# Leftover tap coefficients of a convolution in a two-layer graph network: from a block table to sixteen 32x32 products

## The chip, the cores and the metric

The kernel runs on one core of one Trainium2 chip. The metric is the device time of one execution in microseconds (us). Three runs of the kernel before gave a median of 1967.43 us (1967.24 to 1968.04).

A core has TensorE (PE in the profile, its loads of stationary weights PEld), VectorE (DVE), ScalarE (ACT), GpSimd (POOL) and SyncE (SP). SP computes nothing here: it issues most of the DMA transfers, in the order in which the program gives them, and stands still when one has to wait.

## The reference

Two layers on 128 graphs of 128 nodes with 256 features each, all in float32. The first layer mixes each graph with its adjacency matrix and ends in a layer norm. The second has a branch with two convolutions along the nodes, a message-passing branch, a GRU cell and a layer norm. The change concerns the second convolution, conv2_w with 256 x 256 channels and 17 taps:

```python
xc = jnp.transpose(x, (0, 2, 1))
h = _bn(_conv1d(xc, conv1_w, 0), bn1_g, bn1_b, bn1_m, bn1_v)
h = jax.nn.relu(h)
h = _bn(_conv1d(h, conv2_w, 8), bn2_g, bn2_b, bn2_m, bn2_v)
x_conv = jnp.transpose(jax.nn.relu(h + xc), (0, 2, 1))
```

## The kernel before

**The convolution by frequencies.** The kernel makes the 17-tap convolution from cosine and sine coefficients of length L = 136 (128 nodes and 8 of padding). So there are M = 136 real coefficients for each input and each tap filter: 128 main ones and ML = 8 leftover ones. A table T holds the cosines and sines at the 17 lags, one row a lag, in each quarter of the 128 partitions (rows 0, 32, 64 and 96 on). The coefficients of the filters are W[m] = sum over the taps of T[tap, m] * w[tap], for every pair of input and output channel. They go to memory in w_d, one 512 KB block for each pair of coefficients.

**Stages.** Three stages follow each other.
- The first, up to about 660 us, runs 64 rounds, t = 0 to 63, over pairs of graphs (a_round). A round projects one pair through the first layer (l0_project: f_ps, gate_ps), finishes earlier pairs (gate, norm), runs the first convolution of an older pair (l1_front: conv_ps), takes its coefficients (l1_analyse: coef_ps), turns the next pair's features (l0_turn: xT, adj_ps) and mixes with the adjacency (l0_mix: mix_ps). At its end stand the filter coefficients: a w_unit or a v_unit, or nothing.
- The second loads w_d block by block and multiplies it with the coefficients of the inputs (y_ps, z_ps).
- The third does the rest of the second layer, from synthesis to the GRU (conv2_ps, g_ps).

**Order.** In the first stage the order on TensorE, SP, VectorE, ScalarE and GpSimd is the order of the program text (manual_schedule). PSUM has eight banks, handed out in turn (bank).

**Main units.** A unit u handles four input channels of each of the two input halves, one channel in each quarter of the partitions. w_load(u) loads its taps with four transfers of 64 KB into one of NW = 2 buffers (wt). w_unit(u) makes four products, one in each row group of 32 rows: 17 rows, the 128 main columns of T as stationary weights, 512 moving columns (256 outputs of each half). Four copies on ScalarE empty the four banks into w_o, and w_store writes 1 MB to w_d in the next round. There are NU = 32 units, in rounds 2, 4, ... 32, 33, 35, ... 63; the last one is run after the rounds. The taps for unit u + 2 are loaded in the round after unit u.

**Leftover units.** For the 8 leftover coefficients the taps are loaded a second time. v_load brings FS = 7 input channels with their 17 taps into 119 rows of vt. A block table TL, put together in rounds 3 to 9 by 14 small transfers (leftover_table), has T's eight leftover columns once for each of the 7 channels, on its own 17 rows. v_unit is then one product of 128 rows, 128 columns and 512 moving columns, of which 56 output rows count; VectorE copies them to wl_o, and v_store writes them with two transfers in packets of 2 KB. There are NV = 19 such units, spread over rounds without a main unit.

**What else the prediction names.** SP's list in a round is, in this order: in odd rounds four loads of the next two pairs (xb, load_blocks), one store of the finished features (x_d, x1_store), one load of features (x, load_x), one of the adjacency (adjT, load), the stores of a unit, four loads that bring back the stored features in another layout (x1b, load_back), one store of the turned features (x1T_d, x1T_store), and at the end the taps (w_load). The turn of xb into xT on VectorE is wanted by the next round's f_ps; the turn of x1b into x1T (l1_turn) is wanted by conv_ps.

Of the kernel before, what the change touches and what calls it, by code (L numbers as in the profile page):

```python
# [14 lines left out]
P = 128  # L15
D = 256
# [18 lines left out]
def gnn_layers_kernel(ctx: ExitStack, tc: tile.TileContext, a: dict, out: bass.AP):  # L35
# [53 lines left out]
    FS = P // TAPS  # L89
    TL = taps.tile([P, P], F32, tag="TL", name="TL")  # L90
# [5 lines left out]
    vt = taps.tile([P, 2, D], F32, tag="vt", name="vt")  # L96
# [183 lines left out]
    def way_back():  # L280

        AL = setup.tile([P, P // ML, ML], F32, tag="AL", name="AL")
        nc.vector.tensor_copy(AL, A[:, P:M].unsqueeze(1).to_broadcast([P, P // ML, ML]))
        nc.gpsimd.memset(TL, 0.0)

        nc.gpsimd.memset(vt[96:], 0.0)
        back = setup.tile([P, 1], F32, tag="back", name="back")
        nc.gpsimd.memset(back, 2.0 / L)
        nc.gpsimd.memset(back[0:2], 1.0 / L)
        yield  # L290
        tS = bank("S_ps")
        nc.tensor.transpose(tS[:, 0:P], A[:, 0:P], ident)
        nc.tensor.transpose(tS[:, P : 2 * P], AL.rearrange("p a b -> p (a b)"), ident)
        nc.vector.tensor_scalar(S, tS[:, 0:P], back, None, ALU.mult)
        nc.vector.tensor_scalar(SL, tS[:, P : 2 * P], 2.0 / L, None, ALU.mult)

    def leftover_table(i):

        cols = TL[:, 0 : ML * FS].rearrange("p (r i k) -> p r i k", r=2, i=FS)
        for r in range(2):  # L300
            nc.sync.dma_start(cols[i * TAPS : (i + 1) * TAPS, r, i, :], T[0:TAPS, P + r : M : 2])
# [191 lines left out]
    NV = -(-P // FS)  # L493
    s_v = {}

    def v_set(v):

        return FS * v, min(FS, P - FS * v)

    def v_load(v):  # L500
        f, n = v_set(v)
        nc.sync.dma_start(
            vt[0 : n * TAPS],
            a["conv2_wT"].rearrange("(c f) t o -> (f t) c o", c=NC)[f * TAPS : (f + n) * TAPS],
        )

    def v_unit(v):
        pl = bank(f"wl_ps_{v}")
        nc.tensor.matmul(  # L509
            pl, lhsT=TL, rhs=vt.rearrange("p i (o c) -> p i c o", c=NC), start=True, stop=True  # L510
        )
        ol = s_v[v] = taps.tile([ML * FS, NC * D], F32, tag="wl", name=f"wl_o_{v}")
        nc.vector.tensor_copy(ol, pl[0 : ML * FS])

    def v_store(v):
        ol = s_v.pop(v)
        f, n = v_set(v)
        h = ML // 2
        for r in range(2):
            nc.sync.dma_start(  # L520
                w_d[P // 2 : M // 2, r, f : f + n].rearrange("k f c o -> f k (c o)"),
                ol[r * h * FS : r * h * FS + n * h],
            )

# [41 lines left out]
    units = {2 + 2 * u - 2 * u // NU: u for u in range(NU)}  # L566
    rest = [t for t in range(4 + FS, NP - 1) if t not in units]
    units_v = {rest[v * (len(rest) - 1) // (NV - 1)]: v for v in range(NV)}
# [8 lines left out]
    def a_round(t):  # L577
# [25 lines left out]
        if t + 2 < NP:  # L603
            if 2 <= t + 2:
                load(t + 2)
            if 3 <= t < 3 + FS:
                leftover_table(t - 3)
            if t == FS:
                v_load(0)
# [5 lines left out]
        if t - 1 in units_v:  # L615
            v_store(units_v[t - 1])
            if units_v[t - 1] + 1 < NV:
                v_load(units_v[t - 1] + 1)
# [26 lines left out]
        if 0 <= t < 2:  # L645
            w_load(t)
        if t - 1 in units and units[t - 1] + NW < NU:
            w_load(units[t - 1] + NW)
        if t in units_v:
            v_unit(units_v[t])  # L650
        if t in units:
            if t + 1 < NP:
                w_unit(units[t])

    with tc.manual_schedule(engines={E.PE, E.SP, E.DVE, E.Activation, E.Pool}):
# [5 lines left out]
        w_unit(units[last])  # L661
# [8 lines left out]
        w_store(units[last])  # L670
# [578 lines left out]
```

## Time and profile before

| what | value |
|---|---|
| median of three runs | 1967.43 us |
| profiled execution | 1967.16 us |
| its span, first to last instruction | 1965.4 us |
| granted TensorE clock, mean | 0.997 |
| busy: VectorE, ScalarE, GpSimd | 1501.1, 737.5, 672.8 us |
| w_ps records on TensorE (line 482) | 256 |
| wl_ps records on TensorE (line 509) | 38, 612 ns each (median) |
| copies of w_ps on ScalarE (line 485) | 128, 597 ns each |
| copies of wl_ps on VectorE (line 513) | 19, 670 ns each |
| loads of vt | 18 of 238 KB, 1 of 68 KB |
| stores of wl_o | 36 of 56 KB, 2 of 16 KB |
| loads of wt | 127 of 64 KB, 1 of 34 KB |

A float32 product appears in the profile as two weight loads and two matmul records, its two passes. The records of TensorE overlap, so the busy time of a group is more than what it adds to the span; the distance from the start of one product to the start of the next tells that. In the table of windows a line has the window in us, its length, then for each engine the busy time with the number of instructions in brackets, the granted clock, the busy share of the DMA engines and their GB/s. In the timeline a line has the start, the length from the first to the last of the merged instructions, and their number. The chain of waits follows the work that ended last back from the end. SPq is the instruction stream of SP.

### The profile page before, as it was taken

The page shows a single profiled execution, that of the slowest core. Times are in us where ns is not written, and L with a number is a line of the kernel's source. Part 1 is how long each engine was busy: PE and PEld are TensorE (multiplying, and loading weights), DVE is VectorE, ACT ScalarE, POOL GpSimd, SP SyncE. Part 2 cuts the span into 40 slices and gives each one's busy share as a digit, 9 for nine tenths or more (in the row PEclk, how much of TensorE's full clock was granted, in tenths as well). Part 3 has the DMA queues.
Part 4 walks back from the last instruction along what each step waited for, and adds up shares of the span by engine and source line. Part 5 has one row for each costly group of instructions (what it writes and reads, how often), then busy time and mean ns, then how long its engine had stood idle before and what let it go on. Part 6 is the DMA issues. An engine that isn't in the chain of part 4 may idle for free.

```text
span 1965.4 us, 26741 instructions
## 1 busy us (share of the span) xinstructions
PE 1940.7 (99%) x8539; PEld 1325.4 (67%) x8539; DVE 1501.1 (76%) x3035; ACT 737.5 (38%) x1489; POOL 672.8 (34%) x887
## 2 busy tenths in 40 slices
PE   8999999999999999999999999999999999999997
PEld 5666666666666888866666666666666666666664
DVE  8888888888888644477787777777778777787776
ACT  4666666666666311122223322222222232222222
POOL 2111111111111355544344434434433452543431
PEclk9999999999999999999999999999999999999999
DMA  6787878877786899963212212221221222221100
GB/s 172 204 239 213 238 211 235 242 223 227 217 235 191 278 320 336 313 196 93 66 57 80 82 55 70 72 71 60 82 76 49 72 82 69 62 76 39 43 28 22
DMA packets 334660, 279.90 MB, mean 142 GB/s; under 512 B 150735, under 2 KB 276921, under 8 KB 334521
## 3 DMA queue, kind: packets, MB, share of 16 engines
q1 hardware_dynamic: 327817, 272.68, 45.6%
q10 hardware_dynamic: 6704, 5.52, 0.9%
q8 instruction: 69, 1.13, 0.2%
q14 instruction: 70, 0.57, 0.1%
HBM read 173.26 MB, written 104.86 MB: 142 GB/s over the span
## 4 chain that ended last, share of the span: by engine, by line
PE 93%; DVE 3%; DMA 1%; ACT 1%; issue 1%; POOL 1%; SPq 0%; ACTq 0%; POOLq 0%; DVEq 0%
PE g_ps L1116 43%; PE f_ps L353 11%; PE y_ps L799 5%; PE conv_ps L445 5%; PE gate_ps L358 5%; PE msg_ps L970 4%; PE coef_ps L466 3%; PE conv_ps L916 3%; PE z_ps L812 3%; PE nmp_ps L1048 3%; PE mix_ps L379 3%; PE w_ps L482 2%; PE wl_ps L509 1%; PE conv_ps L923 1%; PE adj_ps L333 1%
## 5 line engine op out<-in xcount | busy, mean ns | idle before, releaser
L318 ACT ACTIVATE y<-y,nb_b,rstd_b 128x256 f32<-128x256 f32 x128 | 70.0, 593 | 561.3 <-DVE nb_b L316 561.3
L353 PE MATMUL f_ps<-w,xT 128*128 128x512 f32 x512 | 244.6, 600 | 2.3 <-DVE xT L423 1.2
L1159 POOL TENSOR_TENSOR u<-u,p 128x512 f32<-128x512 f32 x63 | 79.9, 1269 | 249.1 <-DVE p L1139 240.4
L353 PEld LDWEIGHTS f_ps<-w,xT 128*128 128x128 f32 x512 | 89.1, 189 | 102.8 <-issue 79.8
L1116 PE MATMUL g_ps<-t_h,sh 128*128 128x384 f32 x384 | 156.8, 490 | 0.0
L1116 PE MATMUL g_ps<-t_c,sc 128*128 128x384 f32 x384 | 155.2, 486 | 0.0
L1116 PE MATMUL g_ps<-t_m,sm 128*128 128x384 f32 x384 | 155.2, 486 | 0.0
L358 PEld LDWEIGHTS gate_ps<-w,xT 128*128 128x128 f32 x512 | 97.2, 190 | 68.3 <-issue 53.6
L192 POOL TENSOR_SCALAR rstd_a<-mv_a 128x2 f32<-128x2 f32 x64 | 12.2, 191 | 354.3 <-DVE mv_a L309 249.7
L358 PE MATMUL gate_ps<-w,xT 128*128 128x256 f32 x512 | 131.5, 379 | 0.1
L799 PE MATMUL y_ps<-wb,H 128*128 128x256 f32 x544 | 128.4, 379 | 0.3 <-DMA wb<-w_d 0.3
L807 POOL TENSOR_TENSOR ws<-wb 128x512 f32<-128x512 f32 x67 | 94.4, 1411 | 88.6 <-PE z_ps L812 52.1
L445 PE MATMUL conv_ps<-conv_w,x1T 128*128 128x259 f32 x512 | 122.6, 381 | 0.6 <-DVE x1T L423 0.6
L362 ACT ACTIVATE hom<-f_ps,norm 128x256 f32<-128x256 f32 x128 | 60.6, 473 | 141.4 <-PE f_ps L353 141.3
L799 PEld LDWEIGHTS y_ps<-wb,H 128*128 128x128 f32 x544 | 103.3, 190 | 14.7 <-issue 0.7
L1075 ACT ACTIVATE o<-o 128x1024 f32<-128x1024 f32 (+1 forms) x65 | 67.6, 1040 | 113.7 <-POOL o L1160 54.5
L445 PEld LDWEIGHTS conv_ps<-conv_w,x1T 128*128 128x128 f32 x512 | 97.1, 190 | 16.0 <-PE w_ps L482 1.5
L1116 PEld LDWEIGHTS g_ps<-t_c,sc 128*128 128x128 f32 x384 | 73.0, 190 | 50.9
L1116 PEld LDWEIGHTS g_ps<-t_m,sm 128*128 128x128 f32 x384 | 73.0, 190 | 50.9 <-DVE sm L1064 0.3
L1116 PE MATMUL g_ps<-w_hhT_w,cx1T 128*128 128x384 f32 x256 | 105.1, 492 | 0.0
L1116 PE MATMUL g_ps<-w_ihT_w,nmpT 128*128 128x384 f32 x256 | 103.8, 487 | 1.2 <-ACT nmpT L1052 1.2
L1116 PE MATMUL g_ps<-w_ihT_w,xcT 128*128 128x384 f32 x256 | 103.6, 486 | 1.3 <-ACT xcT L937 1.3
(243 smaller groups left out, 4402.6 us busy)
## 6 DMA issues: line engine op xcount, KB each, us to landing
wb<-w_d SPq DMA_DIRECT2D x68, 512.0 KB
w_d<-w_o SPq DMA_DIRECT2D x32, 1024.0 KB
y_d<-yb SPq DMA_DIRECT2D x68, 256.0 KB
x<-in_x SPq DMA_DIRECT2D x64, 256.0 KB
x_d<-x SPq DMA_DIRECT2D x64, 256.0 KB
cx1T<-x1T_d SPq DMA_DIRECT2D x64, 256.0 KB
yt<-y_d SPq DMA_DIRECT2D x32, 512.0 KB
cx<-x_d SPq DMA_DIRECT2D x32, 512.0 KB
```

The lines of the kernel that those rows point to most:

```text
L318: nc.scalar.activation(dst[:, q, :], src[:, q, :], AF.Identity, bias=nb[:, q : q + 1], scale=rstd[:, q : q + 1],)
L353: nc.tensor.matmul(pf, lhsT=xT[:, c, nodes(j)], rhs=w0[:, c, 0 : 2 * D], start=(c == 0), stop=(c == NC - 1),)
L358: nc.tensor.matmul(pg[:, j * D : (j + 1) * D], lhsT=xT[:, c, nodes(j)], rhs=w0[:, c, 2 * D : 3 * D], start=(c == 0), stop=(c == NC - 1),)
L362: nc.scalar.activation(hom[:, j, :], pf[:, 0:D], AF.Copy, scale=norm[:, j : j + 1])
L379: nc.tensor.matmul(pm[:, j * D : (j + 1) * D], lhsT=adjT_[:, j, :], rhs=hom[:, j, :], start=True, stop=True,)
L445: nc.tensor.matmul(ph[:, 0 : D + CO], lhsT=s["x1T"][:, c, nodes(j)], rhs=conv1_w[:, c, :], start=(c == 0), stop=(c == NC - 1),)
L799: nc.tensor.matmul(py[:, blk, :], lhsT=coefs(blk if k == 0 else 2 * k + 1 - blk, c), rhs=w[:, blk, c, :], start=(c == 0), stop=(c == NC - 1),)
L807: nc.gpsimd.tensor_tensor(ws, w[:, 0], w[:, 1], ALU.add)
L970: nc.tensor.matmul(pm[:, pr * P : (pr + 1) * P], lhsT=s["fh"][i][:, pr, :], rhs=factors["g"][i], start=True, stop=True, skip_group_check=True,
L1075: nc.scalar.activation(rz, rz, AF.Tanh, scale=0.5)
L1116: nc.tensor.matmul(pg[:, lo : lo + 3 * P], lhsT=s[f"f{kind}"][i][:, pr, :], rhs=factors[kind][i], start=(k == 0), stop=(k == 2), skip_grou ...
L1159: nc.gpsimd.tensor_tensor(u4, u2, p5, add)
```

## The change

The leftover coefficients are no longer made from a table TL and taps of their own. They come from the tiles wt that the main units have loaded, for two units (a "set") at once. TL, vt, leftover_table, v_load and v_unit go.

v_set(i) runs sixteen products. For each unit e of the pair and each input half c there is a column group of 32 columns (g); in each row group r, 17 rows of T with its last 32 columns (104 to 135, the eight leftover ones last) are the stationary weights, and the 256 outputs of one half the moving columns. The four column groups of a row group write to the four quarters of the partitions of one bank. Four copies on ScalarE (128x256) bring the banks to wl_o, and v_store writes the eight rows that count of each quarter, with four transfers in packets of 1 KB.

```diff
-    FS = P // TAPS
-    TL = taps.tile([P, P], F32, tag="TL", name="TL")
-    vt = taps.tile([P, 2, D], F32, tag="vt", name="vt")
...
-        nc.gpsimd.memset(TL, 0.0)
-        nc.gpsimd.memset(vt[96:], 0.0)
...
-    def v_unit(v):
-        pl = bank(f"wl_ps_{v}")
-        nc.tensor.matmul(
-            pl, lhsT=TL, rhs=vt.rearrange("p i (o c) -> p i c o", c=NC), start=True, stop=True
-        )
-        ol = s_v[v] = taps.tile([ML * FS, NC * D], F32, tag="wl", name=f"wl_o_{v}")
-        nc.vector.tensor_copy(ol, pl[0 : ML * FS])
+    def v_set(i):
+        po = [bank(f"wl_ps_{i}_{r}") for r in range(Q)]
+        for e in range(2):
+            t = wt[(2 * i + e) % NW].rearrange("p i (o c) -> p i c o", c=NC)
+            for c in range(NC):
+                g = slice(K * (NC * e + c), K * (NC * e + c + 1))
+                for r in range(Q):
+                    k = slice(K * r, K * r + TAPS)
+                    nc.tensor.matmul(
+                        po[r][g, 0:D], lhsT=T[k, M - K : M], rhs=t[k, c], start=True, stop=True
+                    )
+        ol = s_v[i] = taps.tile([P, Q, D], F32, tag="wl", name=f"wl_o_{i}")
+        for r in range(Q):
+            nc.scalar.activation(ol[:, r, :], po[r][:, 0:D], AF.Copy)
+
+    def v_store(i):
+        ol = s_v.pop(i)
+        w = w_d.rearrange("k s (r u) c o -> u c (k s) r o", r=Q)
+        for e in range(2):
+            for c in range(NC):
+                lo = K * (NC * e + c) + K - ML
+                nc.sync.dma_start(w[2 * i + e, c, P:M], ol[lo : lo + ML])
...
-    units = {2 + 2 * u - 2 * u // NU: u for u in range(NU)}
-    rest = [t for t in range(4 + FS, NP - 1) if t not in units]
-    units_v = {rest[v * (len(rest) - 1) // (NV - 1)]: v for v in range(NV)}
+    units = {2 + 2 * u - (u > 10) - (u > 20): u for u in range(NU)}
+    sets = {t + 1: u // 2 for t, u in units.items() if u % 2}
...
-            if 3 <= t < 3 + FS:
-                leftover_table(t - 3)
-            if t == FS:
-                v_load(0)
...
-        if t - 1 in units_v:
-            v_store(units_v[t - 1])
-            if units_v[t - 1] + 1 < NV:
-                v_load(units_v[t - 1] + 1)
+        if t - 1 in sets:
+            v_store(sets[t - 1])
...
-        if 0 <= t < 2:
+        if 0 <= t < NW:
             w_load(t)
-        if t - 1 in units and units[t - 1] + NW < NU:
-            w_load(units[t - 1] + NW)
-        if t in units_v:
-            v_unit(units_v[t])
+        if t in sets and t + 1 < NP:
+            v_set(sets[t])
+            for e in range(2):
+                w_load(2 * sets[t] + NW + e)
         if t in units:
-            if t + 1 < NP:
-                w_unit(units[t])
+            w_unit(units[t])
...
-        w_unit(units[last])
+        v_set(sets[last])
...
-        w_store(units[last])
+        v_store(sets[last])
```

The units now stand in rounds 2, 4, ... 22, 23, 25, ... 41, 42, 44, ... 62, so the last one is inside the rounds. The sets stand in the round after each odd unit: 5, 9, 13, 17, 21, then 24, 28, 32, 36, 40, then 43, 47, 51, 55, 59, and the sixteenth, of round 63, is run after the rounds in the place of the last w_unit. Since a set reads both buffers of taps, the taps of the next two units are loaded after it, eight transfers at once; before, four were loaded after each unit.

## The prediction

> **What bounds the kernel now.** I read the page's shares first, then the slices, then the chain of waits, and last the table of busy time in single rounds.
>
> ```profile
> PE 1940.7 (99%) x8539; PEld 1325.4 (67%) x8539; DVE 1501.1 (76%) x3035; ACT 737.5 (38%) x1489; POOL 672.8 (34%) x887
> PE   8999999999999999999999999999999999999997
> PEclk9999999999999999999999999999999999999999
> ...
> PE 93%; DVE 3%; DMA 1%; ACT 1%; issue 1%; POOL 1%; SPq 0%; ACTq 0%; POOLq 0%; DVEq 0%
> ```
>
> TensorE is busy in every slice at its full clock, and 93% of the chain that ended last is its own work. The change lives in the first stage, up to about 660 us. There the time is a sum of rounds, so I cut out five rounds, each from the first f_ps product of one round to that of the next. The columns are window, length, and then the busy time of each engine.
>
> ```profile
> 163.33:173.45 10.12, 10.12 (x47) 6.53 (x45) 9.04 (x20) 5.39 (x13) 2.07 (x5) 1.00 0.60 172
> 173.45:182.79 9.34, 9.19 (x42) 6.36 (x39) 7.36 (x17) 7.36 (x17) 1.29 (x3) 1.00 0.85 251
> 182.79:192.99 10.20, 10.20 (x46) 6.62 (x46) 9.13 (x21) 5.42 (x14) 2.27 (x6) 1.00 0.64 185
> 192.99:202.92 9.93, 9.93 (x45) 6.90 (x42) 7.94 (x19) 7.39 (x17) 1.48 (x4) 1.00 0.92 273
> 202.92:213.04 10.12, 10.12 (x48) 6.53 (x46) 9.04 (x20) 5.40 (x13) 2.08 (x5) 1.00 0.70 184
> ```
>
> The second round holds neither a main unit nor a leftover unit (call it empty): 9.34 us. The third holds a w_unit: 10.20. The fourth holds a v_unit: 9.93. The first and fifth hold a w_unit after a round with a v_unit: 10.12. TensorE is full in all but the empty one, where it misses 0.15 us. Nothing waits for a DMA here, although the DMA engines are 60 to 92% busy. So the time of this stage moves with what stands on TensorE at the end of a round.
>
> **What is removed.** A v_unit is one 128x512 product in two passes:
>
> ```profile
> 201.15 1.03 PE L379 MATMUL mix_ps<-hom,adjT 128*128 128x256 f32 x4
> 202.02 1.06 PE L509 MATMUL wl_ps<-vt,TL 128*128 128x512 f32 x2
> 202.92 0.59 PE L353 MATMUL f_ps<-w,xT 128*128 128x512 f32 x1
> ```
>
> From its start to the next product is 0.90 us, but it is not worth that. In an empty round TensorE waits about a third of a microsecond for the turned xT before the next f_ps, and the v_unit fills that wait. By pairs of rounds, 9.93 + 10.12 with it against 9.34 + 10.20 without, it costs 0.51 us. Nineteen of them: 19 x 0.51 = -9.7 us. That is all that removal can bring on the path. The copies that go from VectorE (19 of 0.67 us), 19 loads of taps, 38 stores, 14 small table loads and two memsets early in the second round lie beside a full TensorE; I take 0 for them. Their ends: a gain of 0.5 us for the memsets (0.73 us of POOL at 25 us), no loss.
>
> **What is moved.** The 32 units stood in rounds 2 to 63, the last one behind the rounds, in a stretch where TensorE waits anyway (0.61 us idle after it, until x1T is turned). Now the last one stands in round 62, so one more round carries a w_unit: 10.20 - 9.34 = +0.86. In its old place stands the last of the sixteen sets. The gap there is 1.11 us of w_unit plus 0.61 idle, 1.7 in all; a set shorter than that is hidden: 0, and at the most 0.3 if it is the longest below.
>
> **What is added on TensorE.** Fifteen sets in rounds that would be empty, each sixteen products of 17 rows, 32 columns of weights and 256 moving columns. Four row groups, four column groups, two passes each: 32 matmul records. No row of the trace has fewer than 128 columns of weights, so the price has to be bounded. The nearest rows are the products in row groups alone (line 482, then line 1028):
>
> ```profile
> 172.34 1.18 PE L482 MATMUL w_ps<-wt,AT 17*128 17x512 f32 x8
> 173.45 0.70 PE L353 MATMUL f_ps<-w,xT 128*128 128x512 f32 x1
> ```
>
> ```profile
> 978.14 0.73 PE L1028 MATMUL dist_ps<-own,turned 32*128 32x128 f32 x16
> 978.80 0.91 PE L1116 MATMUL g_ps<-t_h,sh 128*128 128x384 f32 x2
> ```
>
> Eight records of 512 columns take 1.11 us until the next product starts. One pass of 512 columns is 0.43 us (four f_ps records in 1.72 us of the chain), so the four row groups run together: 2 x 0.43 = 0.86, and 0.25 for entering and leaving. Against an empty round a w_unit costs 0.86, its two passes and no more, since entry and exit fall into the wait for xT. In the second row each row group has two products, and 16 records of 128 columns (0.108 us a pass, half of the adj_ps pair's 0.22) take 0.66: four passes one behind the other, 0.43, and 0.23 around them. So products of one row group follow each other, where all share the same columns.
>
> A pass of 256 columns is 0.215 us (mix_ps: 0.86 / 4). Taking a set at its streaming time, as the w_unit is:
> - all sixteen tiles together: 2 x 0.215 = 0.43 us;
> - column groups one behind the other, as line 1028 shows for products that share their columns: 8 x 0.215 = 1.72;
> - between them: each row group takes its products in order, the two passes of one product can't overlap, but the first pass of a product runs beside the second pass of the one before it in other columns. Then 2 + 3 = 5 steps: 1.07.
>
> With no overlap at all it would be 32 x 0.215 = 6.9, which both rows exclude. I take 1.07: the rows show that products in different parts of the array overlap and that a row group works in order, and this value keeps both. Fifteen sets: 16.1 us, with ends 6.5 and 25.8.
>
> The Trainium skill, TensorE: Matmul & The Clock Gate (Part 3: Packing small matmuls), reports 10.6 times for sixteen 32x32 tiles of 512 columns; by it a set would take 6.9 / 10.6 = 0.65 us (an estimate from that page), fifteen sets 9.7, and the change would come out at nothing. No row here shows column groups, and the page's case has one pass a product where these have two.
>
> **What is added elsewhere.** Each set has four copies on ScalarE of 128x256 from PSUM (line 363 does this in 0.375 us): 1.5 us a set, at the start of a round whose ScalarE is busy 5.4 of 10.1 us and whose first other work (hom) starts 2.0 us into it. Hidden: 0; if that cover were gone, hom would be late by some tenths, and mix_ps, its reader, stands 8 us later. The Trainium skill, TensorEngine Tiling (Array Packing), PSUM Bottleneck, warns that packing moves the bottleneck to emptying PSUM. Here four w_o copies of 0.6 us already empty a w_unit's four banks in time, so I add nothing for it.
>
> The queue on SP: the two loads of taps for the next pair now wait for the set's last product, at the very end of the round, and everything later on SP stands behind them. One issue takes 0.46 us:
>
> ```profile
> 122.40 1.84 SPq L156 DMA_DIRECT2D wt<-in_conv_wT  x4
> ...
> 132.33 1.91 SPq L126 DMA_DIRECT2D xb<-in_x  x4
> 134.34 0.43 SPq L456 DMA_DIRECT2D x_d<-x  x1
> ```
>
> Eight issues, 3.7 us into the next round; the taps land 2 to 5 us later (2.00 for an x1b load, 5.00 for an x_d store in the chain) and are wanted by the w_unit at 9 us. In ten of the sets the rest of SP's round (x_d, x, adjT, four stores of leftovers in place of two, x1b) ends near 9 us, x1b lands at 11 to 14 and is turned near 13, its conv_ps product stands at 16: no stall. In the five sets of even rounds (24, 28, 32, 36, 40) the four xb loads of the next pair come behind the taps as well. They start at 3.7 us instead of -1, end at 5.6, land at 7.6 to 10.6; VectorE turns xT at 8.4 and TensorE needs it by 9.2. Between 0 and 1.4 us late, five times: 0 to +7. I take 0, from the landing of 2.00.
>
> **Sum.** The profiled execution took 1967.16 us (span 1965.4), the median of the runs is 1967.43, 0.27 above it. -9.7 + 0.86 + 16.1 + 0 = +7.3. From the profiled 1967.16 that is 1974.4; with the 0.27, 1974.7.
>
> **Rivals.**
> *All sixteen tiles run together.* -9.7 + 0.86 + 6.5 = -2.3: 1965.1, not slower. It decides as soon as a set costs less than 0.59 us ((9.7 - 0.86) / 15), the break-even point. For it: tiles share neither rows nor columns pairwise, and four row groups do start together in line 482. Against it: both passes of a product need the same tile, and line 1028 shows a row group working in order.
> *The column groups run one after another.* -9.7 + 0.86 + 25.8 + 0.3 = +17.3: 1984.7. For it: line 1028, the only row in which a row group has several products, is serial. Against: those share all 128 columns.
> *SP's queue decides.* The xb loads come late in the five even rounds, +7 at the most, on top of the least cost of the sets: 1972. For it: the eight issues stand directly ahead of them, and the DMA engines are up to 92% busy. Against: the w_unit that ends those rounds covers 0.8 us of a late xT.
> *The transfers saved bring time.* 4.5 MB of taps less to load. No wait of TensorE in the rounds ends on a DMA; this gives nothing and has no case of its own.
>
> **How the numbers follow.** Order within a row group, columns overlapping (with a set of 0.8 to 1.3 us): 0.40, 1971 to 1979. All together: 0.33. Serial columns: 0.20. SP's queue: 0.07. The likeliest gives 1974.7. The range takes in the two ends of the unknown price, 1965.1 and 1984.7: 1964 to 1985. About 0.2%, 3.9 us, is what a measurement of this kernel can tell from no change. Slower by more: the first case, serial columns, SP's queue, less a little for a set near 0.8: 0.63. All together falls mostly within the bound (0.24), and goes below it with a few gains beside it (0.13).
>
> **What would show it.** In the profile after, the rounds with a set against empty ones: 10.4 us if a set costs 1.07, 9.8 if 0.43, 11.1 if 1.72, and 9.34 still for empty rounds. The matmul records of the sets should start in five steps of about 0.215 us. SP should wait for the set's products ahead of the taps, and f_ps should wait for xT in rounds 25, 29, 33, 37 and 41 no longer than in empty ones; if it does, the queue was mispriced. A stage after 660 us that changes its length would refute the whole account, which leaves it as it was.

## The result and the profile after

The changed kernel takes 1971.45 us (median of 17 runs, 1968.58 to 1973.19), the kernel before in the same series 1967.61 (17 runs, 1966.35 to 1969.25). The ratio is 1.0017, with a 95% interval of 1.0010 to 1.0024: slower by 2 to 4.7 us, a little less than the prediction's bound of 0.2% (3.9 us). The profiled execution took 1969.42 us with a span of 1967.6, so it belongs to the faster half of its kernel's runs.

First the page of the changed kernel: busy times, two rows of the slices, the shares of the chain that ended last, and the group of f_ps products. The last two numbers of that group are the idle time of TensorE right ahead of it, and how much of that ended on xT.

```profile
PE 1937.3 (98%) x9013; PEld 1320.0 (67%) x9013; DVE 1491.3 (76%) x3016; ACT 757.6 (39%) x1553; POOL 671.3 (34%) x885
...
PE   8999999999999999999999999999999999999997
...
PEclk9999999999999999999999999999999999999999
...
PE 89%; DVE 5%; DMA 2%; ACT 1%; issue 1%; POOL 1%; SPq 1%; POOLq 0%; DVEq 0%; ACTq 0%
...
L341 PE MATMUL f_ps<-w,xT 128*128 128x512 f32 x512 | 246.5, 604 | 7.7 <-DVE xT L411 6.6
```

The same group in the kernel before:

```profile
L353 PE MATMUL f_ps<-w,xT 128*128 128x512 f32 x512 | 244.6, 600 | 2.3 <-DVE xT L423 1.2
```

The slices look as before: TensorE full, clock full. But of the chain TensorE has 89% in place of 93, VectorE 5 in place of 3 and DMA 2 in place of 1, and f_ps waits 6.6 us for xT where it waited 1.2. So there are new stalls, and they end on VectorE.

Rounds of the changed kernel, each from its first f_ps to the next round's (columns as in the prediction's windows): an empty round, one with a w_unit, one with a set, the one after the set, and an empty round in trouble.

```profile
153.28:162.61 9.33, 9.18 (x42) 6.35 (x39) 7.35 (x17) 7.37 (x17) 1.29 (x3) 1.00 0.99 289
162.61:172.81 10.20, 10.20 (x46) 6.61 (x46) 9.13 (x21) 5.42 (x14) 2.26 (x6) 1.00 0.54 161
172.81:182.59 9.78, 9.78 (x74) 6.56 (x70) 7.69 (x18) 7.40 (x17) 1.29 (x3) 1.00 0.96 282
182.59:192.82 10.23, 10.23 (x59) 6.64 (x46) 8.90 (x20) 6.58 (x17) 2.26 (x6) 1.00 0.52 143
302.56:313.45 10.89, 9.18 (x42) 6.35 (x39) 7.79 (x18) 7.14 (x17) 1.77 (x4) 1.00 0.80 236
```

The set round is 9.78 us, 0.45 above the empty one, and the w_unit round after it 10.23 instead of 10.20: a set is worth 0.48 us, not 1.07. TensorE is full in it (9.78 of 9.78). The last line is round 30: the same work as the empty round, 9.18 us of busy TensorE, but 10.89 long. The rounds longer than their kind are 24, 26, 30, 34, 38, 42 and 61, by 0.22, 0.19, 1.56, 1.49, 0.52, 0.71 and 0.40 us: 5.1 together. Five of them (26, 30, 34, 38, 42) come two rounds after a set in an even round (24, 28, 32, 36, 40).

The table cuts the profiled executions into pieces, from the starts of f_ps and y_ps. All pieces of this document's kernels after the first y_ps are 1304.3 to 1306.4 us long. The first column varies for a reason that the last section shows.

| kernel | start of round 4 | rounds 4 to 62 | round 63 to the first y_ps |
|---|---|---|---|
| before | 44.46 | 586.69 | 29.47 |
| changed | 43.87 | 589.95 | 29.53 |
| one even set | 46.56 | 586.49 | 29.54 |
| two loads apart | 44.49 | 584.93 | 29.54 |
| leftover stores on ScalarE | 44.21 | 610.92 | 29.54 |
| all odd | 45.59 | 584.55 | 36.10 |
| last set apart | 44.10 | 583.98 | 42.02 |
| all columns | 44.16 | 605.11 | 29.84 |
| products twice | 44.70 | 596.94 | 29.55 |
| before, no unit | 45.38 | 576.76 | 31.65 |
| xb first | 44.59 | 588.60 | 29.55 |
| x1b first | 44.30 | 589.21 | 29.52 |
| one shift | 44.43 | 583.95 | 36.26 |
| copies first | 46.34 | 584.19 | 30.52 |

The change costs 3.26 us in rounds 4 to 62 and nothing after them.

How a stall comes about shows in the timeline around round 30. A line has the start, the length of the merged instructions, their number, and in brackets the idle time ahead with what ended it. SP first; the set of round 28 ends at 292.3:

```profile
292.39 4.38 SPq L153 DMA_DIRECT2D wt<-in_conv_wT  x8
296.87 1.97 SPq L123 DMA_DIRECT2D xb<-in_x  x4
298.93 0.43 SPq L444 DMA_DIRECT2D x_d<-x  x1
...
300.53 3.22 SPq L506 DMA_DIRECT2D w_d<-wl_o  x4
303.87 1.95 SPq L123 DMA_DIRECT2D x1b<-x_d  x4
```

Eight loads of taps, then four of xb, then x_d: the store of x_d goes out 6.5 us later than the first load of taps. Four stores of leftovers follow, and x1b is issued last, at 303.87. VectorE and then TensorE:

```profile
301.49 0.71 DVE L411 STREAM_TRANSPOSE xT<-xb 128x512 f32<-128x512 f32 x1 [0.60 <-DMA xb<-in_x]
...
307.48 0.71 DVE L411 STREAM_TRANSPOSE x1T<-x1b 128x512 f32<-128x512 f32 x1 [2.19 <-DMA x1b<-x_d]
...
312.61 0.70 DVE L411 STREAM_TRANSPOSE xT<-xb 128x512 f32<-128x512 f32 x1
```

```profile
313.45 1.10 PE L341 MATMUL f_ps<-w,xT 128*128 128x512 f32 x2 [1.71 <-DVE xT L411]
```

VectorE stands 2.19 us at the turn of x1b into x1T. It works in order, and ten more instructions stand between that turn and the one of xb into xT. This comes at 312.61, and f_ps has waited 1.71 us. It is not conv_ps, the reader of x1T, that is late; it is the next round's first product, whose input merely stands behind x1T on VectorE.

The sixteen tiles, in the timeline of round 17:

```profile
180.97 1.03 PE L367 MATMUL mix_ps<-hom,adjT 128*128 128x256 f32 x4
181.93 0.73 PE L493 MATMUL wl_ps<-wt,AT 17*32 17x256 f32 x32
182.59 1.13 PE L341 MATMUL f_ps<-w,xT 128*128 128x512 f32 x2
```

From the set's first product to the next f_ps 0.66 us pass, for 32 records of 256 columns. Only 0.45 of them lengthen the round; the rest falls into the wait for xT that an empty round has.

### The profile page after: what moved, and what is told of

Read it like the earlier page. It is cut to its first block, busy times and chain, and to the rows that moved or that the text cites. A ratio compares the mean times of both kernels' runs of the same rounds, so it can differ in the third digit from the quotient of the medians.

```text
span 1967.6 us, 27704 instructions
## 1 busy us (share of the span) xinstructions
PE 1937.3 (98%) x9013; PEld 1320.0 (67%) x9013; DVE 1491.3 (76%) x3016; ACT 757.6 (39%) x1553; POOL 671.3 (34%) x885
## 4 chain that ended last, share of the span: by engine, by line
PE 89%; DVE 5%; DMA 2%; ACT 1%; issue 1%; POOL 1%; SPq 1%; POOLq 0%; DVEq 0%; ACTq 0%
PE g_ps L1090 43%; PE f_ps L341 10%; PE y_ps L773 5%; PE gate_ps L346 5%; PE msg_ps L944 4%; PE conv_ps L433 4%; PE z_ps L786 3%; PE conv_ps L890 3%; PE nmp_ps L1022 3%; PE coef_ps L454 3%; PE mix_ps L367 2%; PE w_ps L470 1%; PE conv_ps L897 1%; DMA x1b<-x_d 1%; SPq L123 1%
## 5 line engine op out<-in xcount | busy, mean ns | idle before, releaser
L433 PEld LDWEIGHTS conv_ps<-conv_w,x1T 128*128 128x128 f32 x512 | 97.1, 190 | 16.1 <-PE wl_ps L493 1.5
L1090 PEld LDWEIGHTS g_ps<-t_h,sh 128*128 128x128 f32 x384 | 71.7, 190 | 48.7
```

What stands on the lines that cost most here:

```text
L433: nc.tensor.matmul(ph[:, 0 : D + CO], lhsT=s["x1T"][:, c, nodes(j)], rhs=conv1_w[:, c, :], start=(c == 0), stop=(c == NC - 1),)
L1090: nc.tensor.matmul(pg[:, lo : lo + 3 * P], lhsT=s[f"f{kind}"][i][:, pr, :], rhs=factors[kind][i], start=(k == 0), stop=(k == 2), skip_grou ...
```

## The experiments

The first account behind the runs: the stalls come from SP's queue after a set, and the sets alone would leave the change near nothing. The rivals are in each expectation.

**One even set.** Only the first of the five even sets stays; the others move to odd rounds, so that no xb loads follow their taps.

```diff
-    units = {2 + 2 * u - (u > 10) - (u > 20): u for u in range(NU)}
+    units = {2 + 2 * u - (u > 10) - (u > 12): u for u in range(NU)}
```

> The two places where the spacing of the units shrinks are put next to each other (after unit 10 and after unit 12), so that only one set, that of round 24, stands in an even round; nothing else differs from the changed kernel. Theory Q (SP's list comes late in the rounds after a set of an even round, where the xb loads stand behind the taps, and the x1b loads behind both): of the stalls after even sets (0.2, 1.6, 1.5, 0.5 and 0.7 us in rounds 26, 30, 34, 38 and 42 of the changed kernel's profile) only the first stays, so 4.3 us less than the changed kernel: 1967.2 us. Rival S (the loss lies in the sets themselves, in their products or their copies on ScalarE, and is spread over all of them): the sixteen sets are all still there, so no change: 1971.4 us. Rival X (only the xb loads matter) gives the same here as Q.

1968.02 us (11 runs), ratio 1.0003 [0.9994, 1.0011]; rounds 4 to 62 fall from 589.95 to 586.49. The stalls two rounds after even sets are gone. What stays are rounds 33 and 34 (1.33 and 0.29 us longer), 33 two rounds after an odd set. There SP stood from 333.0 to 336.1 ahead of x1b, 3.0 us of it put down by the profile to the landing of w_msg, a load on ScalarE's queue. So x1b was late here too: VectorE waited 2.64 us for it, and not for xb.

**Two loads apart.** After the set only the taps of the next unit are loaded; those of the unit behind it follow one round later.

```diff
-            for e in range(2):
-                w_load(2 * sets[t] + NW + e)
+            w_load(2 * sets[t] + NW)
+        if t - 1 in sets:
+            w_load(2 * sets[t - 1] + NW + 1)
```

> After a set only the taps of the next unit are loaded (four transfers); those of the unit after it follow one round later, at the end of SP's list. Sets and units stand where the changed kernel has them. Theory Q: SP is through with the taps 1.9 to 2.2 us earlier, the x1b loads land that much earlier, and VectorE's wait for them (2.2 us in round 30) all but goes: 4 us less, 1967.5 us. Rival S: no change, 1971.4 us. Rival X: the xb loads come 1.9 us earlier too, so the same as Q.

1966.11 us (11 runs), ratio 0.9996 [0.9987, 1.0005]; profiled 1965.41. No round from 4 to 62 is longer than its kind; rounds 29 and 30 here:

```profile
292.53:302.76 10.23, 10.23 (x58) 6.64 (x47) 8.68 (x20) 6.58 (x17) 2.14 (x6) 1.00 0.61 153
302.76:312.09 9.33, 9.19 (x42) 6.36 (x39) 7.32 (x17) 7.35 (x17) 1.28 (x3) 1.00 0.80 242
```

The same sets, the same number of transfers: 5.02 us less than the changed kernel in rounds 4 to 62, and 1.76 less than before. So the whole loss hangs on where the second four loads stand in SP's list. It is the place and not a slower transfer: in round 30, from the first issue of x1b to the turn of x1T, 3.61 us pass in the changed kernel (303.87 to 307.48) and 3.56 here (302.18 to 305.74). The waits between 20 and 640 us show the step in between (engine, line, what it waited for; us in total, times, longest). The changed kernel:

```profile
DVE x1T L411 <- DMA x1b<-x_d: 14.7, 11, 2.2
...
DVE xT L411 <- DMA xb<-in_x: 1.7, 3, 0.6
```

and with the loads apart:

```profile
DVE x1T L411 <- DMA x1b<-x_d: 4.8, 7, 1.0
...
PE f_ps L341 <- DVE xT L411: 0.9, 1, 0.9
```

VectorE still waits for x1b, but at most 1.0 us, and f_ps for xT only once, 0.9 us, ahead of round 4 (no later round is longer than its kind).

**Leftover stores on ScalarE's queue.** This was to take 3.2 us of SP's queue away and leave xb as late as it was.

```diff
-                nc.sync.dma_start(w[2 * i + e, c, P:M], ol[lo : lo + ML])
+                nc.scalar.dma_start(w[2 * i + e, c, P:M], ol[lo : lo + ML])
```

> The four stores of a set go out on ScalarE's queue instead of SP's; all else is the changed kernel. On SP they stand behind the xb loads and ahead of the x1b loads. Theory Q, with the x1b loads as what is late: x1b goes out 3.2 us earlier, its wait is gone, 4 to 5 us less than the changed kernel: 1967 us, unless the four issues (0.7 us each) delay ScalarE. Rival X (the late xb loads are what costs): xb stands where it stood, so no change: 1971.4 us. Rival S: no change either, or worse.

1990.98 us (4 runs), ratio 1.0120 [1.0105, 1.0136]: far above every number that was expected, and nothing learnt about xb and x1b; the "unless" of the expectation came true. ScalarE around 310 us:

```profile
308.41 0.69 ACTq L506 DMA_DIRECT2D w_d<-wl_o  x1
...
309.14 2.09 ACTq L506 DMA_DIRECT2D w_d<-wl_o  x3
311.28 2.07 ACT L473 ACTIVATE w_o<-w_ps 128x512 f32<-128x512 f32 x4 [2.16 <-DMA w_d<-wl_o]
```

The four issues stand in ScalarE's own order, and the copies that empty the banks of the next unit waited 2.16 us for them. A store on ScalarE's queue stops ScalarE while it is issued.

**xb first.** In even rounds with a set the xb loads stand ahead of the taps; x1b was meant to stay as late as it was.

```diff
-        if t > 1 and t % 2 == 1 and t + 1 < NP:
+        if t > 1 and t % 2 == 1 and t + 1 < NP and t - 1 not in sets:
...
             v_set(sets[t])
+            if t % 2 == 0:
+                load_blocks(t + 2, 2)
```

> The changed kernel, but in even rounds with a set the four xb loads of the next pair stand ahead of the eight loads of taps on SP, not behind them; x1b stays where it was, behind all of them. If xb comes late (the prediction's account of the even rounds): the stalls two rounds after even sets (26, 30, 34, 38, 42: 4.4 us together) are gone. If x1b comes late (the trace: the turn of x1T waits for it, and xT stands behind that on VectorE): they stay, 3 to 5 us together.

1969.48 us (one run); rounds 4 to 62 588.60, 1.35 less than the changed kernel. Its waits:

```profile
DVE x1T L411 <- DMA x1b<-x_d: 16.2, 14, 3.1
...
PE f_ps L341 <- DVE xT L411: 4.7, 5, 2.0
```

No turn of xT waits for xb any more (1.7 us in three times in the changed kernel), yet the waits for x1b stay and f_ps still waits 4.7 us; the rounds 26, 30, 34, 38 and 42 are 3.1 us longer together, inside what was expected if x1b decides (rounds 24 and 46 add 0.2 and 0.4). But x1b did not stay where it was. Two of the four xb issues now go out while SP would have waited for the set, and after the sets of rounds 28, 36 and 40 x1b came 0.6 to 0.8 us earlier than in the changed kernel, after those of 24 and 32 it came 0.1 and 1.1 later. Rounds 38 and 42 were free of stalls here, and round 34 lost 2.2 us instead of 1.5. The total alone decides little, then; the single rounds below do.

**x1b first.** The other way round: the leftover stores go behind x1b, which should be issued 3.2 us earlier.

```diff
-        if t - 1 in sets:
-            v_store(sets[t - 1])
         if t + 2 < NP:
             on(t - 2, load_back)
         on(t - 3, x1T_store)
+        if t - 1 in sets:
+            v_store(sets[t - 1])
```

> The changed kernel, but the four stores of the leftovers stand behind the four x1b loads on SP: x1b is issued 3.2 us earlier, xb as late as before. If x1b decides: the stalls two rounds after even sets fall from 4.4 us together to under 1. If xb decides: they stay.

1970.12 us (one run), 589.21 in rounds 4 to 62: of the stalls after even sets only round 34's was left (1.47 us, more than the "under 1" that was expected), but rounds 16, 24, 43, 46, 61 and 62 were longer by 0.2 to 0.8, so that 4.4 us stayed in all. SP around 300 us:

```profile
299.90 0.43 SPq L444 DMA_DIRECT2D x_d<-x  x1
...
300.89 0.50 SPq L118 DMA_DIRECT2D adjT<-in_adjT  x1
302.99 1.81 SPq L123 DMA_DIRECT2D x1b<-x_d  x4
...
305.34 0.72 SPq L506 DMA_DIRECT2D w_d<-wl_o  x1
```

Behind adjT SP stood idle from 301.4 to 303.0: x1b reads back what the x_d store of the same round writes, and waits for that store to land. The leftover stores had partly filled this pause. Counted from the first load of taps x1b came after 9.9 us in place of 11.5, 1.6 earlier and not 3.2, and what holds it up is the place of x_d behind the taps and xb.

The totals of these two runs leave the question open, but the traces settle it round by round. Starts are counted from the first f_ps of the round; a round is compared with the 9.33 us of an empty one.

| kernel, empty round | x1T's turn starts | round longer by |
|---|---|---|
| changed, 26 | 3.55 | 0.19 |
| changed, 30 | 4.92 | 1.56 |
| changed, 34 | 4.85 | 1.49 |
| changed, 38 | 3.88 | 0.52 |
| xb first, 30 | 4.12 | 0.76 |
| xb first, 34 | 5.53 | 2.17 |
| xb first, 38 | 3.26 | 0 |
| x1b first, 30 | 3.22 | 0 |
| x1b first, 34 | 4.83 | 1.47 |
| one even set, 33 | 4.68 | 1.33 |

The loss is the start of x1T's turn less 3.36 us, whether xb stands ahead of the taps or behind them, and nothing where the turn starts earlier. It is so in every empty round from 11 to 61 of these four kernels and of the loads apart but one: in round 61 of x1b first x1T's turn was in time (2.11), the turn of xT waited 0.48 us for xb itself, and the round lost 0.58. So the late x1b makes the stalls, and a late xb could.

**All columns.** On the kernel with the loads apart each product takes 128 columns of weights in place of 32, and so writes all 128 partitions of its bank; the four of a row group overwrite each other.

```diff
-                        po[r][g, 0:D], lhsT=T[k, M - K : M], rhs=t[k, c], start=True, stop=True
+                        po[r][:, 0:D], lhsT=T[k, M - P : M], rhs=t[k, c], start=True, stop=True
```

> The kernel with the two loads apart, but each product of a set has all 128 columns of weights and writes all 128 partitions of its bank, so the four products of a row group overwrite each other: the leftover coefficients come out without meaning. Theory (it is the split by columns that lets the four products of one row group run together): they run one behind the other, 8 x 0.215 = 1.72 a set, rounds with a set 11.0 to 11.1 in place of 9.78, 15 x 1.28 = +19 on the span of 1963.4 of the kernel with the loads apart. Rival (products of one row group pack whatever their columns are, and line 1028 of before was slow for another reason): 9.8.

1985.43 us (one run). The set in round 17 of this kernel:

```profile
185.25 1.03 PE L367 MATMUL mix_ps<-hom,adjT 128*128 128x256 f32 x4
186.21 2.08 PE L493 MATMUL wl_ps<-wt,AT 17*128 17x256 f32 x32
188.22 1.98 PE L341 MATMUL f_ps<-w,xT 128*128 128x512 f32 x4
```

The next f_ps starts 2.01 us after the set's first product; with 32 columns it was 0.66. Set rounds are 11.13 us, a set costs 1.80 + 0.03, and rounds 4 to 62 are 20.2 us longer (15 x 1.35). The four products of a row group do run one behind the other where they share columns, and together where they don't. Loading more weights is not what sets the step: four loads of 128 columns start with the products of the step before, take 0.18 us each and are done ahead of the next step, 0.225 us later (the first step takes 0.33). Starts of the 32 records of one set in ns from the first, loads apart above (round 9), all columns below (round 17):

```
  0   7  14  20  27  34  40  47  54  60  67  74  80  87  94 100 | 255 263 269 ... 338 345 352
  0   7  13  20 | 331 338 347 351 | 557 563 572 576 | 782 ... 1477 | 1683 1690 1698 1702
```

**Products twice.** Each of the sixteen products is done a second time.

```diff
-        for e in range(2):
+        for e in (0, 1, 0, 1):
```

> The kernel with the two loads apart, every product of a set done twice (32 products, the second sixteen overwrite the first with the same values). Theory (a set costs the streaming of its two passes, 0.43): rounds with a set 10.21, +6.5 on 1963.4. Rival (the 0.45 is mostly entry and exit, and the products themselves nearly free): under 9.95. Second rival (the sixteen ran together only by an empty start, and a second round through the tiles queues behind the first in each row group): over 10.4.

1977.91 us (one run). A set of this kernel on TensorE:

```profile
184.15 1.03 PE L367 MATMUL mix_ps<-hom,adjT 128*128 128x256 f32 x4
185.11 1.54 PE L493 MATMUL wl_ps<-wt,AT 17*32 17x256 f32 x64
186.58 1.55 PE L341 MATMUL f_ps<-w,xT 128*128 128x512 f32 x3
```

Set rounds are 10.58: the second sixteen add 0.80 us, more than the first sixteen take from their start to the next f_ps (0.66). The theory's 0.43 is refuted, and the second rival (over 10.4) holds. In the trace most records of the second sixteen start 17 ns apart, from 0.67 us on, those of the first 7 ns apart. So 0.48 is not a price per set that can be multiplied. Why a second round through the same tiles is slower is open.

**Before without its leftover unit.** The kernel before, its table, loads and stores kept, the product and the copy left out (a tile of zeros is stored).

```diff
-        nc.tensor.matmul(
-            pl, lhsT=TL, rhs=vt.rearrange("p i (o c) -> p i c o", c=NC), start=True, stop=True
-        )
-        ol = s_v[v] = taps.tile([ML * FS, NC * D], F32, tag="wl", name=f"wl_o_{v}")
-        nc.vector.tensor_copy(ol, pl[0 : ML * FS])
+        if v == 0:
+            s_v["zero"] = taps.tile([ML * FS, NC * D], F32, tag="wl", name="wl_o_0")
+            nc.gpsimd.memset(s_v["zero"], 0.0)
+        s_v[v] = s_v["zero"]
```

> The kernel before without the products and copies of the leftover unit (its loads, table and stores stay; it stores zeros, so the leftover coefficients are left out). Theory (all that the removal is worth is the product on TensorE, 0.51 a unit): 9.34 for the nineteen rounds, 10.20 for those after them, -9.7, span 1955.7. Rival (part of it is in the loads and stores): less than -7, with the rounds above 9.34.

1959.82 us (one run). Two neighbouring rounds, in the columns of the windows above:

```profile
172.82:182.15 9.33, 9.19 (x42) 6.36 (x39) 7.34 (x17) 7.36 (x17) 1.29 (x3) 1.00 0.89 262
182.15:192.35 10.20, 10.20 (x46) 6.62 (x46) 9.14 (x21) 5.46 (x14) 2.27 (x6) 1.00 0.58 175
```

A round that had a leftover unit is 9.33, the one after it 10.20, and rounds 4 to 62 are 9.93 us shorter than before. The removal is worth what was worked out, and all of it is the product on TensorE with its copy. The span fell by 7.4 only: round 4 started 0.9 later (the clock, see the last section) and the part from round 63 on was 2.2 longer, where conv_ps and y_ps wait 1.55 and 0.99 us; the cause of these waits is open.

**Last unit and last set together behind the rounds.** Could the 0.86 us of the moved unit be had back as well? Four runs with the last w_unit where it stood before and the last set close to it.

*All odd*: unit 30 in round 62, the last unit and set behind the rounds, eight loads as in the change.

```diff
-    units = {2 + 2 * u - (u > 10) - (u > 20): u for u in range(NU)}
+    units = {2 + 2 * u - (u > 30): u for u in range(NU)}
...
-        v_set(sets[last])
+        w_unit(units[last])
+        v_set(sets[last + 1])
```

> The units stand in rounds 2, 4, ... 62 and 63, so that every set of the rounds stands in an odd round (5, 9, ... 61), and the last unit and the last set both run behind the rounds, in the stretch that waits for x1T (1.1 us of w_unit and 0.65 of the set in a gap of 1.7). Theory Q: no stall at all and one w_unit less in the rounds, so against the kernel before -9.7 for the leftover units and 15 sets of 0.48: -2.5, 1965.1 us, faster than both. Rival S (about 5 us of loss spread over the sets): 1970 us.

1972.58 us (7 runs), ratio 1.0027 [1.0016, 1.0038]. The rounds are free of the stalls after even sets (584.55), as the queue's account says of odd rounds; only round 32 is longer, by 0.57 us, and there too x1T's turn is late. But 6.6 us are lost behind them: the unit and the set hold all eight banks, and conv_ps waits 4.0 us for the copies of w_o; these stand behind the gate of the last round until 643.1 and then 1.2 us more for the store of the unit before. The part of the expectation that put the end at nothing was wrong.

*Last set apart*: units as in all odd, loads apart; the last set further back, behind the conv_ps of the last round, its stores right behind it.

> This kernel: units in rounds 2, 4, ... 62 and the last one behind the rounds, as before; all fifteen sets of the rounds in odd rounds; the two loads of taps for the next pair apart by a round; the sixteenth set not beside the last unit but behind the conv_ps products of the last round. Theory (a set costs 0.45 us, the stalls came from SP's queue, the lost tail from eight banks taken at once): -9.7 + 15 x 0.45 = -2.9 and nothing behind the rounds: 1964.5, if the set's banks hold nothing up there. Rival (any product added behind the rounds holds up the stage after, as in the run with both behind them): +5 on that, 1969 to 1971. No stall in any round by either.

1978.97 us (5 runs), ratio 1.0062 [1.0048, 1.0076]. The rival had the direction, and even it was too low. The first product of the next stage:

```profile
670.10 2.47 PE L776 MATMUL y_ps<-wb,H 128*128 128x256 f32 x5 [5.44 <-DMA wb<-w_d]
```

The first load of the next stage's weights waits until the last leftovers are stored (661.98 to 664.90 on SP), and TensorE stands 5.44 us. Before that conv_ps had waited 3.29 us for x1T: its x1b was issued 9.2 us into round 63, in the kernel before 6.2, after SP had stood 3.5 us for the store of x_d.

*One shift*: loads apart, (u > 20) alone, unit 30 in round 61, the set right behind the last unit.

> The two loads of taps apart by a round, and only one shift in the list of rounds (u > 20): unit 30 in round 61, the last unit behind the rounds where it stood before, the sixteenth set right behind it. Theory: in the run with unit 30 in round 62 the w_o copies of the last unit waited for the store of the unit before, and conv_ps for the banks; here that store is out two rounds earlier, as in the kernel before, so the copies start at once and the unit and the set together are late by 0.5 us at the most: 0.86 less than the kernel with the loads apart (span 1963.4), 1962.5 to 1963.0, a ratio of 0.998 to 0.999. Rival (a unit and a set beside each other take all eight banks, whatever the store does): conv_ps waits over 2 us behind the rounds again and the tail gives back 2 us or more, ratio over 1.0005.

1971.88 us (11 runs), ratio 1.0019 [1.0010, 1.0028]: the rival's case. TensorE and ScalarE behind the rounds:

```profile
638.36 0.83 PE L493 MATMUL wl_ps<-wt,AT 17*32 17x256 f32 x32
643.11 3.82 PE L433 MATMUL conv_ps<-conv_w,x1T 128*128 128x259 f32 x8 [3.92 <-ACT w_o L473]
```

```profile
641.95 0.63 ACT L384 ACTIVATE gate<-gate 128x512 f32<-128x512 f32 x1 [4.23 <-DVE gate L383]
642.48 2.04 ACT L473 ACTIVATE w_o<-w_ps 128x512 f32<-128x512 f32 x4
```

The store that the theory blamed was out in time and it did not help: the copies stand behind the gate of the last round in ScalarE's order, and that waits for VectorE until 641.95. conv_ps, with no bank free, starts at 643.11, and at half speed: 3.82 us for eight records that take 1.92 elsewhere, at a granted clock of 0.50 (from 641.6 to 648.5).

*Copies first*: the same, with the unit and the set emitted ahead of the last round's gate.

```diff
+        w_unit(units[last])
+        v_set(sets[last + 1])
         l0_gate(last)
-        w_unit(units[last])
-        v_set(sets[last + 1])
```

> As the run with one shift, but the last unit and the last set are emitted ahead of the gate of the last round, so that their eight copies stand ahead of the gate's exponential on ScalarE (there they stood behind it, and it waited for VectorE until 641.95). Theory (the eight banks were held by copies that stood behind that wait, and by nothing else): copies start at 638.5, two banks are empty by 640, conv_ps starts when x1T is turned, near 641 to 642, and the tail is as long as that of the kernel before, up to 0.5 us more; span 1962.5 to 1963.0, ratio 0.998 to 0.999. Rival (the unit and the set beside each other cost the tail two microseconds wherever their copies stand, because their stores come later or because TensorE's pause lowers its clock): 1965 or more, ratio over 1.000.

The same two engines:

```profile
642.15 1.99 PE L433 MATMUL conv_ps<-conv_w,x1T 128*128 128x259 f32 x8 [0.82 <-DVE x1T L411]
```

```profile
640.59 2.06 ACT L473 ACTIVATE w_o<-w_ps 128x512 f32<-128x512 f32 x4 [0.72 <-PE w_ps L470]
...
643.80 0.63 ACT L384 ACTIVATE gate<-gate 128x512 f32<-128x512 f32 x1
```

The copies start at 640.59, conv_ps waits 0.82 us for x1T and for no bank. The last part is 30.52 us, 5.7 less than with one shift, and the clock stays full there: the order on ScalarE was the cause, of the wait and with it of the half clock. Yet 1967.18 us (11 runs), ratio 0.9997 [0.9988, 1.0006], is no better than the loads apart: 0.74 us fewer in the rounds, 0.98 more behind them. Neither version can be told from the kernel before; against the changed kernel's 1971.45 they are 5.3 and 4.3 us faster. The loads apart have 1.69 us less than before from round 4 to the first y_ps, less than these timings resolve.

## Why the prediction came out as it did

The time lay in the range, 3.3 us under the forecast and on the side foretold, though the 3.84 us between the medians are just inside the 3.9 that the prediction counts as no change. The mechanism was another. Two steps were wrong, in opposite directions, and that they partly cancel is luck: with the price of a set alone put right, the prediction's sum is 1965.8.

- *Where the change lives.* Right: nothing after the first y_ps changed (1304.8 and 1304.3 us).
- *What is removed, -9.7.* Right: 9.93 in rounds 4 to 62 without the products. That the rest of what was removed is worth nothing was not measured apart; the sum below leaves 0.1 us for it.
- *What is moved, +0.86, the last set hidden.* Right: one more round of 10.20, and 29.53 against 29.47 behind the rounds.
- *Fifteen sets at 1.07, +16.1.* Wrong by size: 15 x 0.48 = 7.2. The step that failed was "a row group works in order", taken from line 1028, whose products share all 128 columns. With all columns shared they are serial here too (eight steps, the first of 0.33 us, the others of 0.225); with columns of their own, though the four products of a row group share its rows, all sixteen first passes start within 0.10 us and all second passes within 0.35. The lower end, 0.43, was the right one. The five steps of 0.215 that were named as a sign did not appear. The Trainium skill, TensorE: Matmul & The Clock Gate (Part 3: Packing small matmuls), from which 0.65 us a set was estimated, stood nearer than the row: 0.66 from the first product to the next f_ps, of which 0.48 count. The same section lists weight loads as overlapping running products only where the row group differs; here the weights of four column groups of one row group went in while its products ran (all 32 weight loads start within 0.13 us of the first product, whose record is 0.4 long).
- *Copies on ScalarE, 0.* Right: set rounds of 9.78 and nothing but 0.03 after them.
- *SP's queue, 0 of 0 to +7.* Wrong: +5.0, which the loads apart take away entirely. This is the second step that failed. The bounds held it; the value did not. The working followed xb, asked whether xT would be turned in time, and for the ten odd sets followed x1b too; for the five even sets, where xb adds 2 us ahead of x1b, it did not. That is the case that broke: x1T's turn started up to 4.9 us into the round, and 3.36 is the latest that costs nothing in an empty one. It also asked for conv_ps as the reader of x1T, and not for what stands behind that turn on VectorE. The stalls stood in rounds 26, 30, 34, 38 and 42, one round later than the prediction named them.
- *The sum.* -9.7 + 0.86 + 7.2 + 5.0 = +3.4; measured in rounds 4 to 62: +3.26. The errors were +8.9 and -5.0.
- *The rivals.* "All sixteen together" named the price of a set and lacked the queue; "SP's queue decides" combined the two and gave 1972, with the lowest chance of all. Its transfer was the wrong one, xb in place of x1b.

The median of the changed kernel is 2 us above its profiled execution, while for the kernel before they agree. A part of that is the granted clock: the eight runs whose mean clock is 0.997, as in the profile, average 1970.5 us, the seven at 0.996 and 0.995 lie between 1971.3 and 1973.2. The rest may be longer stalls in other executions, since they hang on the landing of transfers; no run here shows it.

## What to carry to other kernels

A transfer moved to a later place in a queue has to be followed to every transfer behind it, and from each landing to everything that stands behind its reader on an engine that works in order: here four loads too many at one point delayed x1T's turn, and with it the turn of xT behind it that TensorE needed. A row prices another operation only where both share the same limit; products that share columns say nothing about products that don't. And work put behind a loop to hide it needs banks, a place in the copying engine's order, and a store that lands before the next stage reads it; each of the three was short once.

## What the hardware showed beside this

**The clock in the set-up.** In the set-up TensorE is not full (2.00 of the 4 us from 26 to 30 with the loads apart), and in most traces its granted clock falls to half soon after. The length differs from execution to execution, here with one even set and then with the loads apart (the clock is the third number from the end of a line):

```profile
30.00:34.00 4.00, 3.15 (x6) 1.64 (x6) 3.67 (x9) 1.24 (x4) 2.31 (x4) 0.50 0.75 172
34.00:38.00 4.00, 4.00 (x11) 1.35 (x11) 3.64 (x10) 3.31 (x7) 0.29 (x1) 0.50 0.46 113
```

```profile
30.00:34.00 4.00, 3.08 (x6) 1.62 (x6) 3.74 (x9) 1.24 (x4) 2.24 (x4) 0.60 0.75 172
34.00:38.00 4.00, 4.00 (x18) 1.94 (x17) 3.58 (x10) 3.95 (x9) 0.36 (x1) 0.98 0.49 121
```

The first runs at 0.50 for two windows, the second for part of one; round 4 starts at 46.56 and 44.49. The two kernels are alike up to round 4, so this is not the experiment's doing. By the clock records of the traces the half clock lasts 0 us (leftover stores on ScalarE, last set apart; round 4 at 44.1 and 44.2), 3.41 (eight traces, 43.9 to 44.7), 6.83 (all odd, before with no unit; 45.6 and 45.4) or 10.24 (one even set, copies first; 46.6 and 46.3): whole multiples of 3.41. It makes over 2 us between single executions, which is why the pieces from round 4 on are compared here rather than spans. The Trainium skill, TensorE: Matmul & The Clock Gate (Part 1: The HAM clock gate), describes a half clock granted after an idle window of about 3.4 us by a free-running window; the traces agree in the half, in the variation and in the length of a step. Behind the rounds, too, in the run with one shift, the clock fell to half for 6.83 us in a wait of 3.92 us for banks.

**Thirty-two records in 0.35 us.** In a set that follows a full-width product a product starts every 6.7 ns, both passes of all sixteen products have started after 0.352 us, and the next full-width product starts 0.31 us after the last of them, as mix_ps starts 0.31 ahead of the first.
